# Every 1/sqrt of the norms as one GpSimd power in place of a guess and three Newton steps on DVE

## The chip, the cores and the metric

The kernel runs on one core of one Trainium2 chip. A core has TensorE (PE; its weight loads are listed as PEld), VectorE (DVE), ScalarE (ACT), GpSimd (POOL) and SyncE (SP), and 16 DMA engines. Each engine works through its own queue of instructions in order, and waits on semaphores for the others. The metric is the device time of one execution in microseconds (us), as the median of several runs. A profile is one such execution, recorded by the hardware profiler.

## The reference, cut to what matters

The computation is a small gated decoder of two layers on `x` of shape (32, 128, 128), with a context `ctx_1024` of the same shape:

```python
x = x + tanh(g_xattn[0]) * mlstm(layernorm(x), ctx, ctx, ...)      # 8 heads of 16
x = x + tanh(g_ffn[0])   * quantized_ffn(layernorm(x), ...)        # 128 -> 512 -> 128
x = x + tanh(g_xattn[1]) * dtw_align(ctx, layernorm(x))            # dynamic time warping
x = x + tanh(g_ffn[1])   * moe(layernorm(x), ...)                  # 8 experts, 128 -> 512 -> 128

def layernorm(x):
    m = mean(x, -1); v = var(x, -1)
    return (x - m) / sqrt(v + 1e-5)

# at the end of mlstm, over the 16 values of each head:
rrms = rsqrt(mean(h * h, -1) + 1e-6)
h = h * rrms * (1.0 + outnorm_w)
```

So a reciprocal square root is taken of every row of `x` four times, once ahead of each block, and of every head of every row once.

## The kernel before, in words

All 32 samples stay in SBUF as `X`, with the 128 positions of a sample on the partitions. A statistic of a row is thus one column of a small tile: a norm of n samples makes tiles of 128 x n, and the norm of the heads makes 8 columns per sample. The program is written with a tile framework whose scheduler sets the order of the instructions on each engine ahead of time; generators (`yield`) and `tc.issue_after` give it the interleaving. Pools of tiles, each with a number of buffers, set when a tile's memory comes free.

The stages, in order of time:

1. **First norm and gates** (to about 46 us). `first_norm(0)` and `first_norm(1)` norm 16 samples each. `norm_steps` takes `bn_stats` of each sample (L147), joins the halves into a mean and a variance `ve` (L152 to L160), takes the root (`root_steps`, L174 to L182), applies it (`y`, L203, one DVE instruction per sample) and transposes `y` on PE (L207). The transposed rows `YT` feed the gates (L445). On the way to the decays, parts of the gates' running maxima go to DRAM and come back into `RH` by DMAs that SP and POOL issue (L424).
2. **Attention** (to about 177 us). The loop over `p` takes two samples a step: scores on PE, decays (`dm`, ACT, L554), their product on DVE (`sm`, L596 and L591), and values on PE (L606). After steps 4, 8 and 12 a generator `finish` is started for 8 samples, and after 14 and 16 for 4 samples each. It makes `qv` (L645), takes its root `rr` over 8 columns per sample (64 or 32 columns), multiplies the heads by `rr` (L657) and the gain (L662), adds them to `X` (L667), and norms the new `X` for the next block (again `norm_steps`, with 8 or 4 columns). The loop draws three or four steps of this generator after each of its own thirds, so that it lies beside the attention; what remains is drained before the next `finish` starts. The normed rows' largest and smallest values go to `xst` (L499, L500).
3. **FFN, first half** (177 to 221 us). The range of all of `xst` sets a quantization scale, so this stage starts when the last sample is normed. Matmuls, GELU on ACT (L815), two DVE reduces of each block (`hst`, L819 and L820). ACT also prepares the context for the distances (`context_part`, L789 to L793). POOL adds a bias to `X` (L831).
4. **FFN, second half, and distances** (`dense`, 221 to 292 us). Quantize (L865 to L869), matmul (L874), add to `X` (L879). After every second block, `norm_steps` for 8 samples runs beside the next two; its transposed rows give the distances to the context (L884 to L902), which go to DRAM.
5. **Time warping** (292 to 400 us), a chain of DVE scans and compares.
6. **Mixture of experts** (400 us to the end). `aligned(g)` gathers the warped context of 4 samples, adds it to `X` and norms it (4 columns, L1097 applies it). `aligned(0)` and `aligned(1)` come first, the other six beside the first experts' matmuls. Then PE works through all experts (L1164, L1173).

The roots come from `root_steps`, which the diff changes: a guess from the bits of the float, and three Newton steps of three DVE instructions, each of which reads the one before.

Of the kernel before, what the change touches and what calls it, by code (L numbers as in the profile page):

```python
# [8 lines left out]
F32 = mybir.dt.float32  # L9
BF16 = mybir.dt.bfloat16  # L10
I32 = mybir.dt.int32
U8 = mybir.dt.uint8
AF = mybir.ActivationFunctionType
ALU = mybir.AluOpType
# [4 lines left out]
P = 128  # L19
# [19 lines left out]
def tile_flamingo_gated(  # L39
# [21 lines left out]
    nc = tc.nc  # L61

    def pool(stack, name, bufs=1, space=None):
        kw = {} if space is None else {"space": space}
        return stack.enter_context(tc.tile_pool(name=name, bufs=bufs, **kw))

    def new(p, shape, dt, tag, bufs=None):
        kw = {} if bufs is None else {"bufs": bufs}
        return p.tile(shape, dt, tag=tag, name=tag, **kw)

    keep = pool(ctx, "keep")
# [45 lines left out]
    nc.vector.tensor_copy(identb, ident)  # L117
    one_c = new(keep, [P, 1], F32, "one_c")
    nc.gpsimd.memset(one_c, 1.0)
    rev = new(keep, [P, P], F32, "rev")  # L120
    ones = new(keep, [P, P], F32, "ones")
    onesb = new(keep, [P, P], BF16, "onesb")
# [19 lines left out]
    def row_norm_steps(p, v, n, mean, r):  # L142

        m, w = (8, "") if n <= 8 else (16, "_w")
        bn = new(p, [P, m, 6], F32, "bn" + w)[:, 0:n]
        for i in range(n):
            nc.vector.bn_stats(bn[:, i, :], v[:, i, :])  # L147
            if i % 2 == 1:
                yield

        df = new(p, [P, m], F32, "bn_df" + w)[:, 0:n]
        nc.vector.tensor_tensor(df, bn[:, :, 1], bn[:, :, 4], ALU.subtract)  # L152
        ve = new(p, [P, m], F32, "bn_ve" + w)[:, 0:n]
        nc.vector.scalar_tensor_tensor(
            ve, bn[:, :, 2], D * 1e-5, bn[:, :, 5], ALU.add, ALU.add
        )
        nc.vector.scalar_tensor_tensor(mean, df, -0.5, bn[:, :, 1], ALU.mult, ALU.add)
        yield
        nc.vector.scalar_tensor_tensor(df, df, 0.25, df, ALU.mult, ALU.mult)
        nc.vector.scalar_tensor_tensor(ve, ve, 1.0 / D, df, ALU.mult, ALU.add)  # L160
        yield
        for _ in root_steps(p, ve, n, r):
            yield

    def row_norms(p, v, n):
        mean = new(p, [P, 8], F32, "bn_mean")[:, 0:n]
        r = new(p, [P, 8], F32, "bn_r")[:, 0:n]
        for _ in row_norm_steps(p, v, n, mean, r):
            pass
        return mean, r  # L170

    def root_steps(p, v, n, r):

        nc.vector.tensor_scalar(  # L174
            r.bitcast(I32), v.bitcast(I32), -0.5, 1597463007.0, ALU.mult, ALU.add
        )
        m, w = (8, "t") if n <= 8 else (16, "w") if n <= 16 else (64, "u")
        t = new(p, [P, m], F32, "root_" + w)[:, 0:n]
        for _ in range(3):
            nc.vector.tensor_mul(t, r, r)  # L180
            nc.vector.scalar_tensor_tensor(t, v, -0.5, t, ALU.mult, ALU.mult)
            nc.vector.scalar_tensor_tensor(r, t, 1.5, r, ALU.add, ALU.mult)  # L182
            yield

    def norm_steps(p, psp, s0, n, take, tag, shape=None):

        xq = X[:, s0 : s0 + n, :]
        m, w = (8, "") if n <= 8 else (16, "_w")
        mean = new(p, [P, m], F32, "bn_mean" + w)[:, 0:n]
        r = new(p, [P, m], F32, "bn_r" + w)[:, 0:n]  # L190
        for _ in row_norm_steps(p, xq, n, mean, r):
            yield
        for h in range(n // GB):
            if shape is None:
                tp = new(psp, [P, GB, S], F32, tag)
            else:
                if h % 2 == 0:
                    pair = new(psp, shape, F32, tag)
                tp = pair[:, h % 2]
            for i in range(GB):  # L200
                j = GB * h + i
                y = new(p, [P, D], F32, "y", bufs=6)
                got = nc.vector.tensor_scalar(  # L203
                    y, xq[:, j, :], mean[:, j : j + 1], r[:, j : j + 1], ALU.subtract, ALU.mult
                )
                held["y"] = getattr(got, "ins", got)
                nc.tensor.transpose(tp[:, i, :], y, ident)  # L207
                if i % 2 == 1:
                    yield
            take(s0 // GB + h, tp)  # L210
            yield
# [70 lines left out]
    with ExitStack() as st:  # L282
# [3 lines left out]
        hp = pool(st, "heads", bufs=2)  # L286
# [104 lines left out]
        for k in range(6):  # L391
            v = rl if k == 5 else rows[:, k]
# [245 lines left out]
        def finish(s0, n, HN, d2, ms):  # L638

            pr = slice(s0 % 8 // 2, s0 % 8 // 2 + n // 2)  # L640
            HN, d2, ms = HN[:, pr], d2[:, pr], ms[:, pr]

            nc.scalar.activation(d2, d2, AF.Square, bias=small_c, scale=1e-3)
            qv = new(hp, [P, 64], F32, "qv")[:, 0 : 8 * n]
            nc.vector.scalar_tensor_tensor(  # L645
                qv, ms.rearrange("p a x -> p (a x)"), 1.0 / DH, d2.rearrange("p a x -> p (a x)"),
                ALU.mult, ALU.add,
            )
            yield
            rr = new(hp, [P, 64], F32, "rr")[:, 0 : 8 * n]  # L650
            for _ in root_steps(hp, qv, 8 * n, rr):
                yield
            hf = HN.rearrange("p a x e -> p (a x) e")
            hg = HN.rearrange("p a (s h) e -> p (a s) (h e)", h=NH)
            for k in range(n // 4):
                v = slice(32 * k, 32 * k + 32)
                nc.vector.tensor_tensor(  # L657
                    hf[:, v], hf[:, v], rr[:, v].unsqueeze(2).to_broadcast([P, 32, DH]), ALU.mult
                )
                yield  # L660
                v = slice(4 * k, 4 * k + 4)
                nc.vector.tensor_tensor(  # L662
                    hg[:, v], hg[:, v], gain.unsqueeze(1).to_broadcast([P, 4, D]), ALU.mult
                )
                yield
                xv = X[:, s0 + 4 * k : s0 + 4 * k + 4, :]
                nc.vector.tensor_tensor(xv, xv, hg[:, v], ALU.add)  # L667
                yield
            for _ in norm_steps(lp, p_at, s0, n, take, "at"):
                yield  # L670
# [39 lines left out]
        for p in range(B // 2 + 1):  # L710
# [27 lines left out]
            if p in (4, 8, 12, 14, 16):  # L738
                for _ in behind:
                    pass  # L740
                part = 4 if p > 12 else 8
                behind = finish(2 * p - part, part, *tgt)
# [179 lines left out]
    with ExitStack() as st:  # L922
# [51 lines left out]
        for r0, n in CHUNKS:  # L974
# [16 lines left out]
            for r in range(n):  # L991
                u = ru[:, r + 1, 1, 0:S]
# [7 lines left out]
            m = n // 2  # L1000
# [62 lines left out]
    with ExitStack() as st:  # L1063
# [3 lines left out]
        hp = pool(st, "moeh", bufs=3)  # L1067
# [175 lines left out]
```

## Time and profile before

| | us |
|---|---|
| median of 3 runs | 898.74 |
| lowest and highest of the runs | 895.69 to 906.18 |
| profiled execution, its own time | 896.11 |
| span of the profiled execution | 894.3 |
| DVE busy | 555.8 |
| PE busy | 672.0 |
| ACT busy | 379.5 |
| POOL busy | 19.3 |

The span is what the profiler saw between the first and the last instruction; the execution's own time lies 1.8 us above it. A page of the profile has six parts: the busy time of each engine; the span in 40 slices, where a digit is the busy share in tenths; the DMA queues; the chain of work that ended last; the costliest groups of instructions by source line ("L182 DVE ... out<-in, partitions x elements, xcount | busy us, mean ns | idle time of the engine ahead of them and what ended it"); and the DMA issues. The trace can also be asked for its timeline ("start us, duration us, engine line operation") and for busy times in any stretch. "L182" is line 182 of the kernel before.

### The profile page before, as it was taken

What the parts mean: (1) busy time and instruction counts of PE and PEld (TensorE: products, weight loads), DVE (VectorE), ACT (ScalarE), POOL (GpSimd) and SP (SyncE); (2) the same over time, 40 slices, a digit from 0 to 9 for tenths busy, and PEclk for the clock granted to TensorE, in tenths of its full rate; (3) what the DMA queues carried; (4) which work ended last, traced back from release to release, by engine and by line L of the source; (5) the groups of instructions that cost most, each with busy time, mean ns of one, the idle gap of its engine ahead of it and who ended that gap; (6) DMA issues with size and microseconds to landing.
All of it is one profiled execution on the core that took longest, in us unless ns stands there. A gap on an engine that the chain in (4) does not pass through costs nothing.

```text
span 894.3 us, 12616 instructions
## 1 busy us (share of the span) xinstructions
PE 672.0 (75%) x4682; PEld 454.2 (51%) x4682; DVE 555.8 (62%) x1975; ACT 379.5 (42%) x640; POOL 19.3 (2%) x52
## 2 busy tenths in 40 slices
PE   5789997152475000017999999999999999999997
PEld 2245554110353000005777667777777777777776
DVE  7667999889885799786673556995322333222332
ACT  3796875694464000002443444334433334333342
POOL 2000000004000000000000000000000000000000
PEclk9897998555578555556999999999999999999999
DMA  8000000400012535100000000000000000000000
GB/s 314 33 8 6 2 2 2 188 0 0 1 37 58 126 78 120 42 0 1 1 1 1 1 1 1 12 2 24 1 12 1 1 12 1 12 1 1 12 1 12
DMA packets 11943, 25.32 MB, mean 28 GB/s; under 512 B 2386, under 2 KB 7250, under 8 KB 11090
## 3 DMA queue, kind: packets, MB, share of 16 engines
q1 hardware_dynamic: 9880, 20.19, 7.3%
q10 hardware_dynamic: 1874, 4.23, 2.2%
q8 instruction: 36, 0.59, 0.3%
q14 instruction: 25, 0.20, 0.1%
q0 software_dynamic: 128, 0.10, 0.0%
HBM read 14.01 MB, written 4.46 MB: 21 GB/s over the span
## 4 chain that ended last, share of the span: by engine, by line
PE 52%; DVE 22%; issue 2%; ACT 2%; DMA 1%; DVEq 0%; ACTq 0%; POOLq 0%
PE mpo L1173 25%; PE mph L1164 22%; DVE ru L994 3%; DVE hit L1040 3%; DVE hst L819 2%; DVE hst L820 2%; DVE ru L993 2%; DVE bn L147 1%; PE d L888 1%; PE po L874 1%; PE d L890 1%; PE small L1104 1%; DVE pt L1088 1%; PE px L1091 1%; PE px L1100 1%
## 5 line engine op out<-in xcount | busy, mean ns | idle before, releaser
L1173 PEld LDWEIGHTS mpo<-mw2s,hT 128*128 128x128 f32 x2048 | 252.1, 192 | 62.6 <-issue 39.2
L1167 ACT ACTIVATE hT<-mph,mb1s 128x512 f32<-128x512 f32 x256 | 176.0, 687 | 239.3 <-PE mph L1164 237.6
L1173 PE MATMUL mpo<-mw2s,hT 128*128 128x128 f32 x2048 | 256.4, 276 | 0.1
L1164 PE MATMUL mph<-YT,mw1s 128*128 128x512 f32 x512 | 244.5, 600 | 0.0
L1152 DVE SCALAR_TENSOR_TENSOR X<-mpo,GA,X 128x128 f32<-128x128 f32 x192 | 54.0, 343 | 197.9 <-PE mpo L1173 197.9
L1164 PEld LDWEIGHTS mph<-YT,mw1s 128*128 128x128 f32 x512 | 88.0, 193 | 62.6 <-issue 62.5
L1152 DVE SCALAR_TENSOR_TENSOR X<-mb2s,GA,X 128x128 f32<-128x128 f32 x256 | 73.2, 343 | 0.0
L947 PE MATMUL gt_ps<-ident,ru 32*128 32x32 f32 x1 | 0.3, 281 | 78.7 <-DVE ru L994 78.7
L947 PEld LDWEIGHTS gt_ps<-ident,ru 32*128 32x128 f32 x1 | 0.2, 176 | 78.9 <-issue 78.9
L1030 ACT COPY dv<-vv 128x8 bf16<-128x8 bf16 (+1 forms) x5 | 1.1, 220 | 79.0 <-DVE vv L1026 47.6
L554 ACT ACTIVATE dm<-bi 128x512 f32<-128x512 f32 x48 | 28.8, 602 | 11.3 <-issue 4.2
L994 DVE TENSOR_TENSOR_SCAN ru<-ru,dc 64x128 f32<-64x128 f32 x64 | 26.7, 417 | 5.9 <-DMA dc<-d_dram 3.9
L596 DVE TENSOR_TENSOR sm<-sc,dm 128x512 f32<-128x512 f32 x32 | 21.7, 684 | 12.8 <-ACT dm L554 9.8
L810 PE MATMUL ph<-XQ,w1q 128*128 128x512 bf16 x32 | 15.8, 615 | 17.1 <-DVE XQ L801 9.2
L874 PE MATMUL po<-w2q,hqt 128*128 128x128 bf16 x128 | 12.9, 278 | 17.8 <-DVE hqt L869 17.8
L868 ACT ACTIVATE hqt<-HT,low 128x2048 bf16<-128x2048 f32 x8 | 15.8, 1998 | 24.5 <-DVE low L764 14.9
L1101 ACT COPY YT<-px 128x512 f32<-128x512 f32 x8 | 4.7, 586 | 49.6 <-PE px L1100 49.6
L1046 PE MATMUL vt<-ident,vw 64*64 64x64 f32 x1 | 0.3, 310 | 32.3 <-DVE hit L1040 32.3
L1040 DVE SCALAR_TENSOR_TENSOR hit<-jotab,vw,DV 64x128 bf16<-64x128 bf16 x63 | 21.7, 344 | 4.6 <-DMA DV<-dv 2.4
L1181 ACT COPY ye<-mpo 128x512 f32<-128x512 f32 x16 | 9.4, 586 | 35.2 <-PE small L1118 17.8
L510 ACT ACTIVATE qm<-YT,mcol 128x512 f32<-128x512 f32 x32 | 23.1, 727 | 0.0
L147 DVE BATCH_NORM_STATS2 bn<-X 128x6 f32<-128x128 f32 x96 | 22.2, 281 | 0.0
(314 smaller groups left out, 906.8 us busy)
## 6 DMA issues: line engine op xcount, KB each, us to landing
X<-in_x SPq DMA_DIRECT2D x4, 512.0 KB, 6.0
CD<-in_ctx_d SPq DMA_DIRECT2D x4, 512.0 KB, 7.0
CT<-in_ctx_t SPq DMA_DIRECT2D x4, 512.0 KB, 9.2
mw1s<-in_mw SPq DMA_DIRECT2D x1, 2048.0 KB, 7.6
mw2s<-in_mw SPq DMA_DIRECT2D x1, 2048.0 KB, 12.1
out_x<-X SPq DMA_DIRECT2D x8, 256.0 KB, 2.0
d_dram<-dist SPq DMA_DIRECT2D x15, 128.0 KB, 2.4
rblk<-ru ACTq DMA_DIRECT2D x6, 297.0 KB, 4.8
```

The costliest lines, as they stand in the source:

```text
L147: nc.vector.bn_stats(bn[:, i, :], v[:, i, :])
L510: nc.scalar.activation(held["qm", g][:, h], YT[:, GB * g : GB * g + GB, :], AF.Copy, scale=mcol[:, h : h + 1],)
L554: done = nc.scalar.activation(dm, bi, AF.Exp)
L596: got = nc.vector.tensor_tensor(sm, scs[:, u], dm, ALU.mult)
L819: nc.vector.tensor_reduce(hst[:, 0, o : o + 1], hb, AX.X, ALU.max)
L874: nc.tensor.matmul(po[:, i, :], lhsT=hq[:, c, i * S : (i + 1) * S], rhs=w2q[:, c, :], start=(c == 0), stop=(c == NC - 1),)
L994: nc.vector.tensor_tensor_scan(ru[:, r + 1, 0, 1 : S + 1], u, dc[:, r, :], BIG, ALU.min, ALU.add)
L1040: nc.vector.scalar_tensor_tensor(hit, jotab[0:H2], vw[:, r + 1 : r + 2], DV[:, r, :], ALU.is_le, ALU.mult, accum_out=vw[:, r : r + 1],)
L1152: nc.vector.scalar_tensor_tensor(X[:, b, :], v, gate, X[:, b, :], ALU.mult, ALU.add)
L1164: nc.tensor.matmul(ph, lhsT=mw1s[:, e, c * P : (c + 1) * P], rhs=tok, start=True, stop=True)
L1167: nc.scalar.activation(hT[:, c, :], ph, AF.Gelu_apprx_tanh, bias=mb1s[:, e, c : c + 1])
L1173: nc.tensor.matmul(po[:, i, :], lhsT=hT[:, c, i * S : (i + 1) * S], rhs=mw2s[:, e, c, :], start=(c == 0), stop=(c == NC - 1),)
```

## The change

`root_steps` becomes a single GpSimd instruction, a tensor-tensor power with a constant tile of -0.5 as exponent. The tile is set once at the start. The scratch tiles `root_t`, `root_w` and `root_u` go, and the generator yields once where it yielded three times, so the steps that the loops draw from it shift.

```diff
     one_c = new(keep, [P, 1], F32, "one_c")
     nc.gpsimd.memset(one_c, 1.0)
+    mhalf = new(keep, [P, 64], F32, "mhalf")
+    nc.gpsimd.memset(mhalf, -0.5)
...
-        for _ in root_steps(p, ve, n, r):
+        for _ in root_steps(ve, r):
             yield
...
-    def root_steps(p, v, n, r):
-
-        nc.vector.tensor_scalar(
-            r.bitcast(I32), v.bitcast(I32), -0.5, 1597463007.0, ALU.mult, ALU.add
-        )
-        m, w = (8, "t") if n <= 8 else (16, "w") if n <= 16 else (64, "u")
-        t = new(p, [P, m], F32, "root_" + w)[:, 0:n]
-        for _ in range(3):
-            nc.vector.tensor_mul(t, r, r)
-            nc.vector.scalar_tensor_tensor(t, v, -0.5, t, ALU.mult, ALU.mult)
-            nc.vector.scalar_tensor_tensor(r, t, 1.5, r, ALU.add, ALU.mult)
-            yield
+    def root_steps(v, r):
+
+        nc.gpsimd.tensor_tensor(r, v, mhalf[:, 0 : v.shape[-1]], ALU.pow)
+        yield
...
             rr = new(hp, [P, 64], F32, "rr")[:, 0 : 8 * n]
-            for _ in root_steps(hp, qv, 8 * n, rr):
+            for _ in root_steps(qv, rr):
                 yield
```

## The prediction

> **What bounds the kernel now.** I read the page first: the busy shares, the busy tenths, the chain that ended last. No engine bounds all of it, so a saving on DVE is worth what the stage around it pays for DVE.
>
> ```profile
> span 894.3 us, 12616 instructions
> PE 672.0 (75%) x4682; PEld 454.2 (51%) x4682; DVE 555.8 (62%) x1975; ACT 379.5 (42%) x640; POOL 19.3 (2%) x52
> ...
> PE   5789997152475000017999999999999999999997
> ...
> DVE  7667999889885799786673556995322333222332
> ...
> PE 52%; DVE 22%; issue 2%; ACT 2%; DMA 1%; DVEq 0%; ACTq 0%; POOLq 0%
> ```
>
> POOL, which receives the new work, is busy for 2% of the span. Next, the busy time by stage, with stretches that I cut at the phase borders (us; busy PE, PEld, DVE, ACT, POOL; clock, DMA share, GB/s):
>
> ```profile
> 83.00:152.00 69.00, 61.10 (x960) 33.11 (x956) 64.67 (x224) 48.45 (x96) 0.00 (x0) 0.98 0.01 2
> 152.00:177.00 25.00, 7.95 (x85) 5.21 (x84) 20.35 (x86) 13.83 (x63) 0.00 (x0) 0.57 0.43 169
> 221.00:292.00 71.00, 40.84 (x243) 30.04 (x243) 52.83 (x200) 35.37 (x41) 1.12 (x7) 0.69 0.16 34
> 424.00:894.00 470.00, 462.39 (x2681) 338.03 (x2679) 211.14 (x863) 186.10 (x274) 0.00 (x0) 1.00 0.02 5
> ```
>
> From 83 us, where the first `finish` starts, to 152 us DVE is busy for 94%: the attention is paced by DVE. From 424 us on PE is (98%), so nothing that DVE gives up there can count. Between them the norms lie on latency chains. Third, the groups by form, for the prices:
>
> ```profile
> L182 DVE SCALAR_TENSOR_TENSOR rr<-root_u,rr 128x64 f32<-128x64 f32 x9 | 2.0, 221 | 0.2
> L182 DVE SCALAR_TENSOR_TENSOR bn_r<-root_t,bn_r 128x8 f32<-128x8 f32 x21 | 3.3, 159 | 0.2
> L831 POOL TENSOR_TENSOR X<-X,b2g 128x1024 f32<-128x1024 f32 x4 | 9.3, 2346 | 143.0 <-ACT aa L849 143.0
> L352 POOL TENSOR_TENSOR wkv<-wg 128x16 f32<-128x16 f32 x1 | 0.2, 221 | 1.5 <-DMA wg<-in_ifg_w 1.5
> ```
>
> The Newton steps hardly depend on width: 159 ns for 8 columns, 221 for 64. POOL's cost does. Its two adds give (2346-221)/(1024-16) = 2.1 ns a column on about 0.19 us fixed. Last, the timeline, for one exposed root and one that is trapped:
>
> ```profile
> 406.88 0.16 DVE L174 TENSOR_SCALAR bn_r<-bn_ve 128x4 int32<-128x4 int32 x1
> ...
> 408.77 0.16 DVE L182 SCALAR_TENSOR_TENSOR bn_r<-root_t,bn_r 128x4 f32<-128x4 f32 x1
> 408.97 1.11 DVE L1097 TENSOR_SCALAR y<-X,bn_mean,bn_r 128x128 f32<-128x128 f32 x4
> 409.37 1.24 PE L1100 MATMUL px<-ident,y 128*128 128x128 f32 x4 [5.71 <-DVE y L1097]
> ```
>
> ```profile
> 272.65 0.17 DVE L174 TENSOR_SCALAR bn_r<-bn_ve 128x8 int32<-128x8 int32 x1
> ...
> 275.75 1.12 DVE L897 TENSOR_SCALAR dd<-d,aa 128x128 f32<-128x128 f32 x4 [1.92 <-PE d L890]
> ...
> 278.73 2.15 DVE L203 TENSOR_SCALAR y<-X,bn_mean,bn_r 128x128 f32<-128x128 f32 x8
> ```
>
> In the first, ten dependent steps hold PE off for 2.1 us. In the second, three Newton steps queue behind `dd`, which waits for PE, and a 2 us root takes 6.1.
>
> **What the Trainium skill says.** "GPSIMD Engine Reference", 2.1: each instruction goes through two software dispatches, and a two-input body has a floor of about 2.5 cycles per element; at the 1.2 GHz of its section 1 that is 2.1 ns, and the adds agree. Its section 7 puts a dependent fp32 chain at 4 cycles a step, and 3.1 puts a body of three or more operations at about 3 per cycle; no row here shows either. No page prices a power. "SBUF — State Buffer", § SBUF: two separate sides: POOL and a DVE instruction with two SBUF inputs lock each other out for a whole instruction; no row of before shows it. "Perfetto Trace Analysis", § GPSIMD Engine Instruction, calls POOL's profiled spans unreliable, so I judge a power by when its reader starts.
>
> **The change part by part.** There are 24 roots: 2 of 16 columns (first norm), 3 of 64 and 2 of 32 (`finish`), 3 of 8 and 2 of 4 (the norms in `finish`), 4 of 8 (dense), 8 of 4 (`aligned`). Removed: 24 x 10 = 240 DVE instructions. Added: 24 POOL powers, and one memset in POOL's idle first microsecond, at no cost.
>
> Price of a power: T(n) = 0.2 + c n us, 0.2 from the 221 ns row. For c I guess that log2, product and exp2 take 60 operations. Fully overlapped at 3 per cycle that is 20 cycles, 17 ns; one dependent chain at 4 cycles each is 240 cycles, 200 ns. Both are estimates from the "GPSIMD Engine Reference" sections above. I take c = 40 ns: partly overlapped, below the middle because columns are independent. Crossings to and from POOL: a memset on POOL (L983) starts 0.14 us after the DVE `dd` that it waits for, and a DVE memset starts as the POOL memset before it (L989) ends, so 0.2 us for both. The reader's latency L = T + 0.2 is then 0.56 (4), 0.72 (8), 1.04 (16), 1.68 (32), 2.96 us (64).
>
> What DVE does meanwhile decides. In the changed kernel's order, DVE has at most one `wtmp` or `sm` (0.3 to 0.6 us) between `qv` and `HN*rr`, nothing between `bn_ve` (L160) and `y` in the attention, two `bn_stats` (0.5 us) in the first dense norm. DVE works in order, so the rest of L is a stall, and behind it queue the next `sm` (L596/L591), for which PE's value matmuls (L606) wait. The saved steps are counted by the time that they cost on DVE, what is interleaved taken off.
>
> - *First norms (12.9 to 46 us).* Ten steps took 15.01-12.91 = 2.1 us twice; L(16) = 1.04. The first gain reaches the gates; part of the second meets the wait for `sp`. Take -1.8. POOL's two indirect loads of `RH` (L424) are queued behind both powers, done by about 26 us; they wait for `m_dram`, written after 34.66, so they are not delayed.
> - *Two full batches (83 to 136 us).* A 64-column root costs 3.51 us between L174 and `HN`, less two `sm` of 0.6: 2.3. The 8-column one costs 1.8. The power costs 2.96-0.5 and 0.72. Each batch -0.9, both -1.8; the third 64 column root +0.15. With c = 40 the wide roots lose what the narrow ones win.
> - *End of the attention (146 to 175 us).* Five roots there are partly hidden in each other now; by the same count 6.8 us of DVE. Stalls: 0.72 + 0.56 + 0.56 and one L(32) = 1.68; the other is covered by `sm` and four reduces. That is -3.3, of which I give back 1.3 because the last two `finish` are no longer interleaved. -2.0.
> - *First FFN half (177 to 221 us).* No root; DVE's `hst` reduces bound it. Some of ACT's `context_part` moves in from before it; ACT has 44-33.6 = 10 us of room. 0; without that room, up to 4.
> - *Dense (221 to 292 us).* POOL's bias adds (L831) stay ahead of these powers and end at 221 us, before the first norm. Roots interleaved with `bn_stats` were nearly free, but `y` follows `bn_ve` directly now instead of 4 to 6 us later, and the last norm's 6.1 us becomes about 1. PE needs 3.7 us for each pair's distances, which takes part of it. -3.0. What is late next is PE's L888/L890.
> - *`aligned(0)` (406.9).* 2.1 becomes L(4) less one `pt`: -1.7; later ones run beside PE's matmuls: 0. If a power took over 2 us there, `y` would be late for PE.
>
> Sum: -1.8-1.8+0.15-2.0-3.0-1.7 = -10.2 us. The profiled execution took 896.11 us (span 894.3, 1.8 around it), giving 885.9; the median, 898.74, lies 0.3% above, giving 888.5. I predict 887.
>
> **Rivals.**
> - *Power dear, slower.* One mechanism: the in-order stall of DVE at `HN*rr` behind a wide power. At c = 170, L(64) = 11.3 and L(32) = 5.8: +8.5 per 64-column root and its narrow neighbour, three times (25), +7 in the end of the attention (both 32-column stalls exposed), +1.5 first norms, dense 0, -1.1 `aligned`: +33, 930 us. It decides from c about 80, where the sum crosses zero. For it: POOL's columns come one after another, and a power is long. Against: its add already runs at its port floor.
> - *Wash.* c of 45 to 100: 891 to 907. For it: the wide and narrow roots nearly cancel at my own price.
> - *Power cheap.* c = 20 gives L(64) = 1.7: -5.7 batches, -3 end, -2.3 first norms, -3.3 dense, -1.8: -16, 881 us. The attention cannot give much more: p-steps without `finish` take about 5.2 us (48.86 to 53.72, 79.33 to 84.70, between `sm` of L591) against 6.4 now, a limit of 4.8 a batch.
> - *DVE off the path* (only chains count): first norms, dense and `aligned` alone, about -6.5: 891. Against: DVE at 94%.
>
> **How the numbers follow.** About 1% is what a measurement of this kernel tells from no change. The forecast's case, c below 45, has 0.46 (0.15 of it the cheap power), the wash 0.16 and DVE off the path 0.05, together 0.21, the dear power 0.33. Range: from 878 (c near 17) to 925 (c near 155), leaving out a tenth or so above and little below; the forecast's own is 879 to 892.
>
> **What would show it.** L174 becomes a POOL TENSOR_TENSOR x24: right if the gap from `qv` to `HN` on DVE, less `sm`, is 2 to 3 us for 64 columns and if DVE's idle time before L203 shows POOL for 0.3 to 0.8 us each. `y` of the last dense norm should start within 1.5 us of `bn_ve`, PE's first `mph` should come 1.7 us sooner after `ends`, and the stretch from 424 us should keep its length. Wrong if `HN` waits over 5 us for POOL, or if POOL's spans grow with width at above 80 ns a column.

## The result, and the profile after

The changed kernel is slower. Its median of four runs is 942.41 us (938.19 to 943.91), against 901.59 us (895.69 to 906.18, four runs) for the kernel before on the same chip. The ratio on record is 1.0485, 95% interval 1.044 to 1.0529; the two medians as they stand give 1.0453, within it. The profiled execution took 941.07 us, its span 939.4: 45.1 us more than the span before. Lines from L184 of the kernel before stand six lower in the numbers of the changed one (`sm` L590 and L585, `HN` L651, `y` L197 and L1091); the power is L176.

The page of the changed kernel, busy times, busy tenths and the chain that ended last:

```profile
span 939.4 us, 12422 instructions
PE 687.9 (73%) x4682; PEld 459.5 (49%) x4682; DVE 521.2 (55%) x1735; ACT 379.6 (40%) x640; POOL 89.4 (10%) x77
...
PE   5789668634337600001889999999999999999998
...
DVE  6564645656987569978544255799223223223232
...
PEclk9895779655557755555799999999999999999999
...
PE 58%; DVE 26%; POOL 7%; ACT 4%; issue 3%; DMA 1%; ACTq 0%; POOLq 0%; DVEq 0%
```

DVE gave up 34.6 us of work and POOL took on 70.1, and POOL now holds 7% of the chain, where it had nothing. DVE's row shows what that did: after the first slices it was at 8 and 9 before, and is at 4 to 6 now, so DVE is idle for nearly half of the very stage that it paced. The powers, from the groups by form (out<-in, count | busy us, mean ns | idle time ahead):

```profile
L176 POOL TENSOR_TENSOR rr<-qv,mhalf 128x64 f32<-128x64 f32 x3 | 31.8, 10595 | 42.5 <-DVE qv L639 42.5
L176 POOL TENSOR_TENSOR bn_r<-bn_ve,mhalf 128x8 f32<-128x8 f32 x7 | 11.5, 1637 | 80.3 <-DVE bn_ve L162 80.3
L176 POOL TENSOR_TENSOR rr<-qv,mhalf 128x32 f32<-128x32 f32 x2 | 10.9, 5428 | 8.5 <-DVE qv L639 8.5
L176 POOL TENSOR_TENSOR bn_r<-bn_ve,mhalf 128x4 f32<-128x4 f32 x10 | 10.1, 1007 | 135.8 <-DVE bn_ve L162 135.8
L176 POOL TENSOR_TENSOR bn_r_w<-bn_ve_w,mhalf 128x16 f32<-128x16 f32 x2 | 5.8, 2916 | 14.5 <-DVE bn_ve_w L162 14.5
```

Five widths on one straight line: (10595-1007)/(64-4) = 160 ns a column, and 0.37 us fixed. The timeline at the first `finish` (start us, duration us, engine, line, operation, and in brackets the wait ahead of it), DVE and then POOL:

```profile
87.48 0.21 DVE L639 SCALAR_TENSOR_TENSOR qv<-ms,d 128x64 f32<-128x64 f32 x1
87.62 0.41 DVE L266 TENSOR_SCALAR wtmp<-wtmp 128x512 f32<-128x512 f32 x1
98.51 0.69 DVE L651 TENSOR_TENSOR HN<-HN,rr 128x512 f32<-128x512 f32 x1 [10.47 <-POOL rr L176]
```

```profile
87.78 10.69 POOL L176 TENSOR_TENSOR rr<-qv,mhalf 128x64 f32<-128x64 f32 x1 [16.19 <-DVE qv L639]
```

POOL starts 0.09 us after `qv` and `HN` 0.04 us after the power: the hand-over is as cheap as forecast, and nearly the whole length of the power, 10.47 of 10.69 us, is DVE's idle time. DVE's waits for POOL over the span (total us, times, longest):

```profile
DVE HN L651 <- POOL rr L176: 36.3, 4, 10.5
...
DVE y L197 <- POOL bn_r L176: 13.4, 9, 1.8
...
DVE y L1091 <- POOL bn_r L176: 9.2, 8, 1.2
```

Four of the five wide powers are waited for. The first one of 32 columns runs beside an `sm` and four reduces and ends at 189.99 us, and `HN` follows at 190.03 without idle time of DVE.

And the busy time by stage, in the stretches that answer to those shown of before (us; busy PE, PEld, DVE, ACT, POOL; clock, DMA share, GB/s):

```profile
87.50:191.00 103.50, 75.16 (x1015) 38.92 (x1015) 57.32 (x162) 49.24 (x96) 42.12 (x7) 0.76 0.01 2
191.00:216.30 25.30, 5.42 (x64) 4.10 (x64) 13.06 (x44) 9.47 (x38) 7.44 (x3) 0.57 0.24 93
262.30:333.00 70.70, 40.81 (x243) 29.12 (x243) 48.49 (x160) 35.34 (x41) 7.83 (x10) 0.72 0.14 30
465.00:939.00 474.00, 462.42 (x2681) 337.46 (x2679) 200.90 (x801) 186.10 (x274) 6.04 (x6) 1.00 0.02 5
```

The attention's stretch went from 69 to 103.5 us for about as many matmuls (1015 recorded, 960 before), with DVE at 55% instead of 94%, and the granted TensorE clock in it went from 0.98 to 0.76. The other stages moved little.

### The profile page after: what moved, and what is told of

It reads as the page before. It is cut to its first block, busy times and chain, and to the rows that moved or that the text cites. A ratio compares the mean times of both kernels' runs of the same rounds, so it can differ in the third digit from the quotient of the medians.

```text
span 939.4 us, 12422 instructions
## 1 busy us (share of the span) xinstructions
PE 687.9 (73%) x4682; PEld 459.5 (49%) x4682; DVE 521.2 (55%) x1735; ACT 379.6 (40%) x640; POOL 89.4 (10%) x77
## 4 chain that ended last, share of the span: by engine, by line
PE 58%; DVE 26%; POOL 7%; ACT 4%; issue 3%; DMA 1%; ACTq 0%; POOLq 0%; DVEq 0%
PE mpo L1167 24%; PE mph L1158 21%; POOL rr L176 4%; DVE ru L988 3%; DVE hit L1034 2%; POOL bn_r L176 2%; DVE hst L813 2%; DVE hst L814 2%; DVE ru L987 2%; PE sc L524 1%; PE d L882 1%; DVE bn L149 1%; DVE y L197 1%; PE at L600 1%; PE at L439 1%
## 5 line engine op out<-in xcount | busy, mean ns | idle before, releaser
L548 ACT ACTIVATE dm<-bi 128x512 f32<-128x512 f32 x48 | 28.7, 600 | 47.3 <-issue 34.0
L176 POOL TENSOR_TENSOR rr<-qv,mhalf 128x64 f32<-128x64 f32 (+1 forms) x5 | 42.6, 8528 | 51.0 <-DVE qv L639 51.0
L176 POOL TENSOR_TENSOR bn_r<-bn_ve,mhalf 128x4 f32<-128x4 f32 (+1 forms) x17 | 21.5, 1266 | 216.1 <-DVE bn_ve L162 216.1
L600 PE MATMUL at<-sm,va 128*32 128x64 f32 x512 | 16.2, 250 | 28.1 <-DVE sm L590 28.0
L590 DVE TENSOR_TENSOR sm<-sc,dm 128x512 f32<-128x512 f32 x32 | 21.8, 684 | 16.4 <-ACT dm L548 12.7
L988 DVE TENSOR_TENSOR_SCAN ru<-ru,dc 64x128 f32<-64x128 f32 x64 | 26.6, 416 | 4.7 <-DMA dc<-d_dram 2.6
L600 PEld LDWEIGHTS at<-sm,va 128*32 128x32 f32 x512 | 10.2, 122 | 35.7 <-DVE sm L590 26.4
L651 DVE TENSOR_TENSOR HN<-HN,rr 128x512 f32<-128x512 f32 x8 | 5.5, 690 | 36.3 <-POOL rr L176 36.3
L197 DVE TENSOR_SCALAR y<-X,bn_mean,bn_r 128x128 f32<-128x128 f32 x64 | 17.8, 341 | 13.4 <-POOL bn_r L176 13.4
L524 PE MATMUL sc<-qm,CD 64*128 64x256 f32 x128 | 24.7, 490 | 0.0
```

Source lines behind the costliest of these rows:

```text
L176: nc.gpsimd.tensor_tensor(r, v, mhalf[:, 0 : v.shape[-1]], ALU.pow)
L197: got = nc.vector.tensor_scalar(y, xq[:, j, :], mean[:, j : j + 1], r[:, j : j + 1], ALU.subtract, ALU.mult)
L524: nc.tensor.matmul(scs[:, k, 4 * v : 4 * v + 4], lhsT=CD[kr, n, :], rhs=qm[kr, :, n % GB, SH:S], start=True, stop=True,)
L548: done = nc.scalar.activation(dm, bi, AF.Exp)
L590: got = nc.vector.tensor_tensor(sm, scs[:, u], dm, ALU.mult)
L600: last = nc.tensor.matmul(at[HW * c : HW * c + HW, v, k, t], lhsT=w, rhs=m, start=True, stop=True)
```

## The experiments

Besides the theory of the *stall* (DVE stands in order behind powers that are long), three rivals were put to the chip: the *trip* (each hand-over to POOL costs, whatever it computes), the *order* (one yield in place of three moves what follows a root), and later the *clock* (PE's gaps let its clock fall). Ratios are to the kernel before in the same group of runs.

**Half of the change each.** Powers for the wide roots alone, then for the norms alone; the other roots keep the Newton steps and their three yields.

```diff
-        for _ in root_steps(ve, r):                  # wide roots only
+        for _ in newton_steps(p, ve, n, r):
```
```diff
-            for _ in root_steps(qv, rr):             # norms only
+            for _ in newton_steps(hp, qv, 8 * n, rr):
```

> Power on GpSimd for the five wide roots of finish alone (64 and 32 columns); the 19 norms keep the guess and the three Newton steps on DVE. Theory 'stall' (DVE waits in order at HN*rr for a power of 0.37 us + 0.159 us a column, so the wide roots carry the loss): +25 to +35 us, ratio 1.028 to 1.039; HN waits about 10.4 us three times and 5.6 us at least once, as with all powers. Rival 'order' (fewer steps between yields shift the norms against PE and ACT): about half the loss, 1.015 to 1.025. Rival 'trip' (each of the 24 hand-overs to POOL and back costs about 2 us, whatever the power lasts): 5 of 24, +9 us, 1.010.

> The other half: powers for the 19 norms (4, 8 and 16 columns), Newton steps on DVE for the five wide roots. 'Stall': +3 to +10 us, ratio 1.003 to 1.011: about +1.6 in the first norms (2.9 us power against 2.1 us of steps), +4 in the expert phase where y comes late for PE, -1 at the first aligned, the rest near zero. 'Order': 1.015 to 1.025. 'Trip': 19 of 24, +36 us, 1.04.

Wide roots only: 939.83 us, ratio 1.0465 (1.0428 to 1.0503), as much as the whole change and more than the stall had allotted (1.039 at most). Norms only: 913.36 us, 1.0167 (1.0131 to 1.0204), more than it had allotted, and in the order's range. That rules out the trip, which wanted 1.010 and 1.04. But the halves add up to more than the whole, so something is missing from this account. It lies in the attention: in the profiles that stage is longer than before by 39.1 us with the wide roots, by 10.7 with the norms and by 38.9 with both. DVE's order is not the same in the three kernels, and what the missing part is stays open.

**A cheap operation in the same place.**

```diff
-        nc.gpsimd.tensor_tensor(r, v, mhalf[:, 0 : v.shape[-1]], ALU.pow)
+        o = mhalf[:, 0 : v.shape[-1]]                # mhalf is 1.0 here
+        nc.gpsimd.tensor_tensor(r, v, o, ALU.mult) if v.shape[-1] < 32 else nc.gpsimd.tensor_tensor(r, v, v, ALU.subtract)
```

> Same instructions in the same places on POOL, but with a cheap operation in place of the power: a product with 1.0 for the norms, a difference v - v for the wide roots (so the norms scale by the variance and the attention's output is multiplied by zero: that part of the computation is replaced). POOL should take 0.2 to 0.35 us each. 'Stall': the loss goes and the sum of my own price list for a cheap power appears: -10 to -16 us, ratio 0.982 to 0.989. 'Order': 1.02 or more stays. 'Trip': about 1.04 stays.

876.37 us, ratio 0.9766 (0.9742 to 0.979), span 873.3: faster than before by more than I had expected. The order of DVE's instructions is that of the changed kernel, and so are the hand-overs; only the length differs. The groups of this kernel:

```profile
L177 POOL TENSOR_TENSOR bn_r<-bn_ve,mhalf 128x4 f32<-128x4 f32 x10 | 2.0, 201 | 137.9 <-DVE bn_ve L162 137.9
L177 POOL TENSOR_TENSOR bn_r<-bn_ve,mhalf 128x8 f32<-128x8 f32 x7 | 1.4, 204 | 80.3 <-DVE bn_ve L162 80.3
L177 POOL TENSOR_TENSOR rr<-qv 128x64 f32<-128x64 f32 x3 | 1.0, 329 | 38.8 <-DVE qv L640 38.8
L177 POOL TENSOR_TENSOR rr<-qv 128x32 f32<-128x32 f32 x2 | 0.5, 239 | 8.5 <-DVE qv L640 8.5
L177 POOL TENSOR_TENSOR bn_r_w<-bn_ve_w,mhalf 128x16 f32<-128x16 f32 x2 | 0.4, 219 | 15.2 <-DVE bn_ve_w L162 15.2
```

The 24 operations take 5.3 us here and 70.1 us as powers: 64.8 us more on POOL. The span of the changed kernel is 939.4-873.3 = 66.1 us longer. Stage by stage (ends read from the timelines: first `sm`, the range of the normed rows `xs`, `ends`, first `mph`, end of the span; the FFN's first half takes 46 us in all three and stands in the third row):

| stretch | before | cheap operation | power | power less cheap, span | power less cheap, on POOL |
|---|---|---|---|---|---|
| to the first `sm` | 47.3 | 45.9 | 49.9 | +4.0 | +5.4 |
| attention, to `xs` | 127.5 | 116.8 | 166.4 | +49.6 | +47.1 |
| FFN, distances, warping, to `ends` | 225.5 | 219.9 | 225.9 | +6.0 | +5.7 |
| to the first `mph` | 13.7 | 11.9 | 12.7 | +0.8 | +0.8 |
| experts | 480.3 | 478.8 | 484.5 | +5.7 | +5.6 |

The last column is the count of powers in the stretch times the difference of the mean durations (attention: 3 x 10.27 + 2 x 5.19 + 3 x 1.43 + 2 x 0.81). Stage by stage, the span grows by about as much as POOL's work. In the attention this is a balance of several parts, and not the waiting alone. DVE's waits for POOL grow there by 41.6 us, from 2.4 to 44.0. Another 3.6 of the 49.6 us arise ahead of the first `qv`, where no power runs (37.6 us from the first `sm` to `qv` against 34.0): there the clock stands at 0.50 from 70.3 us to that `qv` at 87.5, and in the kernel with the cheap operation only from 65.5 to 72.3. Why it stood there longer is not shown.

The removed steps, the new order and the hand-overs, with 5.3 us of cheap operations, are together worth -21 us; the length of the powers, with all that it sets off, is worth +66; the sum is the +45 that was measured. (In the cheap kernel the norms scale by other numbers and the attention adds zeros. The instructions do not take other times for it: added up form by form, those of DVE and ACT last 1024.8 us with the powers and 1026.7 us with the cheap operation.)

**The order alone.** Newton steps everywhere, with one yield behind all ten instructions; then with three yields behind them.

```diff
             nc.vector.scalar_tensor_tensor(r, t, 1.5, r, ALU.add, ALU.mult)
-            yield
+        yield                                        # one; or: for _ in range(3): yield
```

> No power at all: guess and three Newton steps on DVE, but with one yield after all ten instructions, where the changed kernel has its one yield (before: one after each step). The order of the other work is then that of the changed kernel. 'Stall' and 'trip': within 0.4% of before. 'Order': +20 to +40 us, ratio 1.02 to 1.04.

> Newton steps as one block of ten instructions as in the kernel with one yield (ratio 1.0165 there), but three yields behind them, so that all that follows a root keeps the place of before. 'Order' (the loss of the one-yield kernel comes from what follows a root moving two places forward): 0.996 to 1.004. 'Block' (ten dependent DVE instructions in a row hold up sm): 1.012 to 1.02 stays.

One yield: 911.91 us, 1.0165 (1.0094 to 1.0236), which the stall had not expected. Its four runs took 905.84, 906.89, 916.92 and 918.54 us, with mean granted clocks of 0.853, 0.855, 0.839 and 0.842; the profile is that of 916.92. Three yields: 900.04 us, 1.0019 (0.9999 to 1.0039). So the ten instructions in a row cost nothing that can be told, and two yields fewer cost about 15 us, with no power in sight. That is what an order can do, not what the changed kernel's order does: in the traces DVE's order in the one-yield kernel differs from that of the changed kernel, from the first norm's `y` on, against what the expectation says. The changed kernel's own order is the one of the cheap kernel, and there nothing was lost.

How the one-yield kernel loses shows in the stretch from one `HN*rr` to the next (before, then one yield):

```profile
88.70:113.30 24.60, 22.46 (x356) 12.26 (x359) 22.82 (x75) 18.23 (x37) 0.00 (x0) 1.00 0.01 2
```

```profile
89.70:123.00 33.30, 31.96 (x338) 16.25 (x339) 23.63 (x76) 18.75 (x36) 0.00 (x0) 0.69 0.01 1
```

About the same work of DVE and ACT, and somewhat fewer matmuls, but PE is busy for 32 us instead of 22 at a clock of 0.69 instead of 1.00. From 94.0 to 114.5 us the clock is at 0.50 with PE busy nearly all the time, so PE paces the stage there. In "TensorE: Matmul & The Clock Gate" of the Trainium skill, Part 1, the clock is at half after at least one idle window of about 3.4 us. The trace agrees with the half, but PE was not idle: it was busy for 0.95, 0.60, 0.65 and 0.82 of the four microseconds ahead of the fall. The kernel before had nearly the same dip (0.60, 0.78, 0.79, 0.80 and 0.69 from 90 to 95 us), and its clock stayed at 1.00. So how idle PE must be for a fall is not shown.

**Keeping PE busy.** The one-yield kernel with small groups of idle matmuls (nobody reads what they write) ahead of the value matmuls next to `HN*rr`:

```diff
+            if held.pop("warm", None):               # set beside HN*rr, n == 8
+                for _ in range(8 // (2 if u == 2 else 1)):
+                    nc.tensor.matmul(to, lhsT=identb, rhs=src, start=True, stop=True)
```

> The one-yield Newton kernel (ratio 1.0165) with three small groups of idle matmuls (about 0.8 us each, into the accumulator that the value matmuls then overwrite) in each full batch, ahead of the value matmuls that stand beside HN*rr, where PE's busy share dipped to 0.6 just before its clock fell to a half. 'Clock' (the loss of that kernel is matmuls at half clock): the clock stays at 1.0 from 88 to 123 us, the batch is 25 to 28 us in place of 33, ratio 1.000 to 1.009. 'Order' as such, without the clock: 1.0165 or more, since PE has 2.5 us a batch more to do.

912.19 us, 1.0145 (1.0103 to 1.0188): no gain in all. But in the first batch, where DVE's order is the same but for the places of one `sm` and one small `bn_df`, the forecast of the clock came true: 26.2 us from `HN` (88.43) to `HN` (114.64) in place of 33.3, at full clock. In the second batch the clock fell all the same, from 128.2 to 145.2 us. The two stretches:

```profile
89.70:116.00 26.30, 25.05 (x378) 13.81 (x368) 22.93 (x76) 19.02 (x37) 0.00 (x0) 1.00 0.01 2
```

```profile
126.00:150.00 24.00, 22.38 (x231) 12.22 (x237) 12.54 (x37) 12.56 (x26) 0.00 (x0) 0.64 0.01 1
```

So the half clock is what the one-yield kernel lost by in its first batch; with the fill, the fall came in the next one.

**The clock's and the order's part in the changed kernel.** Three kernels were to put idle matmuls into PE's gap behind a 64-column power, and one gave the power three yields.

```diff
+                for _ in range(48):                  # and 128 in the last of the three
+                    nc.tensor.matmul(at[:, :, u, SH:S], lhsT=identb, rhs=..., start=True, stop=True)
```
```diff
         nc.gpsimd.tensor_tensor(r, v, mhalf[:, 0 : v.shape[-1]], ALU.pow)
-        yield
+        for _ in range(3):
+            yield
```

> The changed kernel with 24 idle matmuls (128x512 bf16, about 5 us at full clock, their output is read by nobody) on PE behind each of the three 64-column powers, in the gap in which PE waits for sm. DVE's wait stays. Theory 'stall and clock' (the wait empties PE for 6 us, the granted TensorE clock falls to a half, and the matmuls of the next 6 to 12 us then take twice as long): HN still waits 10.4 us for POOL, the clock stays near 1.0 behind the wait, a batch takes 31 to 33 us in place of 36, the total is 8 to 15 us under the changed kernel: ratio to before 1.031 to 1.039. 'Stall alone': as the changed kernel, 1.045 to 1.053, batches of 36 us.

> The fill of idle matmuls again, placed so that nothing holds it: the changed kernel with 48 idle matmuls (128x128 bf16, about 5 us) into the part of the accumulator that the value matmuls then overwrite, right ahead of the value matmuls that wait for the sm behind HN*rr, three times. (In the first try the fill waited for a free accumulator, whose reader was stuck behind HN on DVE, so it ran after the gap.) 'Stall and clock': HN still waits 10 us, PE's gap is filled, the clock stays above 0.9 in the 12 us behind it, a batch takes 31 to 33 us in place of 36, total 8 to 15 us under the changed kernel, ratio to before 1.031 to 1.040. 'Stall alone': 1.044 to 1.053.

> As the fill of 48 idle matmuls in PE's gap, with 128 of them: 48 took 2.84 us at full clock and left 7.5 us of the gap open, behind which the clock fell to a half as before. 128 take 7.6 us at full clock, 13.7 at half clock. 'Stall and clock': at the first batch, where PE enters the gap at full clock, the gap is under 2 us, the clock stays at 1.0 behind it, and the stretch from HN to the next HN is 30 to 33 us (37.9 with the short fill, 36.0 in the changed kernel); where PE enters it at half clock the fill itself costs up to 4 us. 'Stall alone': 36 us or more in every batch.

> The changed kernel with three yields behind each power, as many as the Newton steps had, so that what follows a root keeps its place of before. The Newton kernel lost 1.65% with one yield and nothing that can be told with three. If that loss by order is part of the changed kernel's: 8 to 15 us less than the changed kernel, ratio to before 1.031 to 1.040. If the waits for POOL swallow it: as the changed kernel, 1.044 to 1.053.

The fills gave 956.9 us (1.0651, 1.0611 to 1.069), 952.88 (1.0603, 1.0557 to 1.0649) and 961.58 (1.0699, 1.0642 to 1.0756), all worse than the change, and none isolates the clock. The first ran behind the gap, the second ended 7.5 us before the gap did. The third filled the first gap (the matmuls run from 93.20 to 100.97), and the clock, at 0.50 from 70.3 us, rose to 1.00 at 94.2 and stayed there to 107.8. But the order changed too: two `sm` that had stood ahead of the eight-column power and `y` now stand behind them, as if the planner that lays out the order had counted the fill. PE waited 5.7 us for the first of these, and the batch took 42 us. This remains inconclusive: how much of the +45 the half clock carries is not shown. An estimate of the most that it can be: in the attention PE is busy for 114.7 us in the changed kernel and for 95.4 with the cheap operation, for the same matmuls, so about 19 us, if all of it were on the path.

Three yields on the power: 939.37 us, 1.0464 (1.0431 to 1.0497). That cannot be told from the changed kernel, so beside these waits the two yields gain nothing that shows.

**Hiding the power.** If the wait is the loss, a power with enough DVE work beside it should pay. In the first two batches `HN*rr` is put behind later `sm`, Newton steps stay everywhere else.

```diff
+            for _ in range(14 if late else 0):       # late: the first two batches
+                yield
...
+                with tc.issue_after(held["sm"]):
                     nc.vector.tensor_tensor(hf[:, v], hf[:, v], rr[:, v]..., ALU.mult)
```

The second try splits each of these powers, the third adds the norm's root:

```diff
+                for k in range(2):
+                    for _ in root_steps(qv[:, 32 * k : 32 * k + 32], rr[:, 32 * k : 32 * k + 32]):
+                        yield
...
+                for _ in range((10, 8)[k] if late else 0):   # ahead of HN*rr of half k
+                    yield
...
-                for _ in range(3 if p < 13 else 4):
+                for _ in range(4):
```
```diff
+        for _ in root_steps(ve, r) if far else newton_steps(p, ve, n, r):   # far: these batches
+            yield
+        for _ in range(4 if far else 0):
+            yield
...
+                    if far:
+                        tie.enter_context(tc.issue_after(held["sm"]))       # ahead of each y
```

> Newton steps on DVE for all but the first two 64-column roots; for these two the power on GpSimd, with 14 more empty steps between the power and HN*rr, and HN*rr put behind the newest sm on DVE, so that DVE has about 10 us of other work while POOL computes. 'Stall' (the loss is the waiting, not the power): HN waits under 2 us, the power still takes 10.6 us, the two batches shorten to 22 to 24 us (24.6 and 25.3 before), total -2 to -5 us, ratio 0.994 to 0.998. Rival 'disturbance' (POOL's 10.6 us at SBUF slow DVE's own instructions beside it): sm and y beside the power grow by over 10%, ratio 1.003 or more.

> The hiding of the first two 64-column powers done better: each as two powers of 32 columns, ten empty steps ahead of the first HN*rr half, eight more ahead of the second, four steps a turn in place of three, each HN*rr put behind the newest sm; Newton steps everywhere else. In the first try HN still waited 3.3 and 2.8 us and the clock fell behind both waits. 'Stall': HN waits under 1 us each, no fall of the clock between 84 and 130 us, both batches at 22.5 to 24.5 us (24.6 and 25.3 before), total -2 to -6 us, ratio 0.993 to 0.998. If the batches are no shorter although nothing waits for POOL, the ten steps that a power saves were not on the path: 0.998 to 1.004.

> The kernel with the two hidden wide roots (0.9967), and in the same two batches the 8-column norm as a power too, with y put behind the newest sm. It takes ten more DVE instructions (1.8 us) from each batch and adds a power of 1.64 us, of which one sm (0.7 us) covers a part. If DVE's time bounds these batches: another -1 to -3 us, ratio 0.993 to 0.996. If y waits out the power on the path instead: 0.997 to 1.001.

The first try gave 903.6 us, 1.0031 (1.001 to 1.0053): `HN` still waited 3.3 and 2.8 us, and the clock fell behind both. As halves of 32 columns, further apart: 895.33 us, 0.9967 (0.9948 to 0.9987). `HN` waited 1.1 us at most, but in the profiled execution (span 894.2) the batches are longer, not shorter (29.1 and 26.6 us from `HN` to `HN`), with the clock at 0.50 from 103.0 to 116.6 us; where the 0.3% comes from stays open. With the norm's root of these batches as a power too: 889.53 us, 0.991 (0.9879 to 0.9941), span 888.0: 0.9% less than the kernel before. Its powers, and its stretch from 84 to 137 us, with that of the kernel before under it:

```profile
L178 POOL TENSOR_TENSOR rr<-qv,mhalf 128x32 f32<-128x32 f32 x4 | 21.7, 5434 | 14.7 <-DVE qv L657 14.7
L178 POOL TENSOR_TENSOR bn_r<-bn_ve,mhalf 128x8 f32<-128x8 f32 x2 | 3.3, 1636 | 12.4 <-DVE bn_ve L162 12.4
```

```profile
84.00:137.00 53.00, 50.60 (x836) 27.97 (x836) 45.85 (x130) 40.65 (x82) 22.40 (x6) 1.00 0.01 2
```

```profile
84.00:137.00 53.00, 49.40 (x795) 27.00 (x789) 49.04 (x163) 40.67 (x81) 0.00 (x0) 1.00 0.01 2
```

A power of the same columns costs what it cost in the changed kernel, now beside a DVE that is busy for 87% of the stretch and a PE at full clock. DVE has 3.2 us less to do there than in the kernel before. So a power beside which DVE has other work need not cost anything; in the changed kernel it was the wait that cost. That the powers are what puts this kernel ahead of the one before is not shown: it also draws four steps a turn and puts `HN*rr` and `y` behind `sm`, and the same order with Newton steps was not run. Between the second and the third try the clock differs as well (no fall from 66.0 to 144.5 us in the third).

## Why the prediction was wrong, step by step

- **The price of a power.** The step that failed is the term c: taken as 40 ns a column, measured 160. Five widths give T(n) = 0.37 + 0.16 n us. The bounds, 17 to 200 ns, held, and the measured price lies near the end of one dependent chain. I had put the value below the middle "because columns are independent", with nothing in the profile behind it. With it the reader of 64 columns was to be held up for 2.96 us; DVE stood for 10.5, 10.1 and 10.1 us. The mechanism, DVE waiting in order behind the power, was the forecast's own; its size was not. Both signs that I had named for being wrong came: `HN` waited over 5 us, and the spans grew by more than 80 ns a column. The sum crossed zero at c = 80, well inside the bounds, so the sign was open and I gave it 0.33.
- **Crossings of 0.2 us**: right, 0.09 and 0.04 us. So was the reading of the order: only `wtmp` lies between `qv` and `HN`, and `y` follows `bn_ve` with nothing between.
- **First norms, -1.8**: measured +2.6 to the first `sm`. `y` waited 3.0 us twice where ten steps had taken 2.1.
- **Full batches, -0.9 each**: from `qv` to `qv`, 36.2 and 35.5 us after against 25.0 and 25.3 before. The dear rival had said +8.5 a batch; it was +11.2 and +10.2. Where the other two microseconds come from is argued, not shown: that rival let DVE gain all of the saved steps, but once DVE stands for 10 us it paces nothing, and other waits come up (`sm` for ACT's `dm`, 12.7 us in all against 9.8 before). The clock is also at 0.50 from 128.3 to 141.9 us, beside and behind the second gap; its share stays open.
- **Third 64-column root, +0.15**: from its `qv` to the next, 25.1 us against 14.1, so +11.0, by the same stall.
- **End of the attention, -2.0**: from there to the range `xs`, 32.1 us against 27.7, so +4.4. That one of the two 32-column powers would be covered was right; `HN` waited 5.6 us for the other. With the cheap operation it is 22.1 us, -5.5.
- **FFN, first half, 0**: right, 46.0 us in both.
- **Dense, -3.0**: measured +0.4 from there to `ends`. The cheap operation shows -5.7 here, and the powers add 6.1.
- **`aligned(0)`, -1.7**: -1.0, the difference being a power of 1.0 us in place of 0.36.
- **The other `aligned`, 0**: wrong, +4.2. I had said that a power of over 2 us would make `y` late for PE; 1.0 us was enough. PE's waits for `y` in the first expert's stretch, before and after:

```profile
PE px L1100 <- DVE y L1097: 2.4, 6, 0.5
```

```profile
PE px L1094 <- DVE y L1091: 6.5, 6, 1.2
```

PE already waited for each `y` before, so the chain from statistics to `y` was on PE's path there in spite of PE's 98%: its waits for `y` grew by 4.1 us, and the stage by 4.2.
- **Rivals.** "Power dear" named the mechanism, place and sign; its 930 us against 942 lacks the expert stage and two to three microseconds a batch, and it had both 32-column stalls exposed. "Power cheap" (881) is nearly the kernel with the cheap operation (876). "DVE off the path" fell: with DVE idle in the attention, the stage grew by 38.9 us. Not among the rivals was that the TensorE clock might fall beside a wait on DVE, as it did in the second batch.
- **A slip**: the loads of `RH` on POOL's queue are four plain ones, not two indirect ones.

## What to carry to other kernels

Moving work to an idle engine is free only if its consumer has something else to do meanwhile: ask first how many microseconds of other instructions lie between the producer and the reader on the reader's in-order engine, and price the new operation per column before anything else. When a price has bounds that differ by ten and the sum changes sign between them, the sign is not known, whatever value is taken. In a stage where PE is nearly full, look at the granted clock beside the busy shares: a thinner stretch can cost more than itself when the matmuls behind it run at half clock, as in the first batch of the one-yield kernel.

## What the runs showed of the hardware

- A power on GpSimd takes 0.37 us + 0.16 us a column on 128 partitions (1.01, 1.64, 2.92, 5.43 and 10.60 us for 4, 8, 16, 32 and 64 columns); a product or difference in the same place takes 0.20 to 0.33 us. POOL's recorded spans were a sure guide here: in all 24 cases the reader starts 0.03 to 0.04 us after the recorded end.
- A power did not keep DVE from SBUF. "SBUF — State Buffer", § SBUF: two separate sides, has POOL and a DVE instruction with two SBUF inputs lock each other out for a whole instruction. The trace does not agree for a power. In the kernel with the hidden norms the first two powers of 32 columns run from 81.44 us for 10.87 us, and within the second of them these ran at their usual length, 0.69 us:

```profile
88.21 0.68 DVE L683 TENSOR_TENSOR HN<-HN,gain 128x512 f32<-128x512 f32 x1
88.92 0.69 DVE L688 TENSOR_TENSOR X<-X,HN 128x512 f32<-128x512 f32 x1
```

- A granted clock of 0.50 about doubles a matmul's time: in the first fill (24 idle matmuls), matmuls of 128x512 bf16 in a row start 427 ns apart at 0.50 and 216 ns apart at 1.00.
- Two yields in a generator, which change no instruction, moved the time by 1.5%: behind a dip of PE to between 0.60 and 0.95 for four microseconds its clock was at 0.50 for the next 20.5 us, with PE busy nearly throughout. Nearly the same dip left it at 1.00 in the kernel before.
